# Eight-layer network on one core: a third product block on GpSimd, runs of 32 tokens in the recurrence, and the expert choice in three pieces

## The chip, the cores and the metric

The kernel runs on one core of a Trainium2 chip. Times are device microseconds of one execution of the whole program; less is better.

## The reference

The program computes four layers on a tensor `x` of 4 images, 128 channels and 64 x 64 pixels. Each layer adds a token mixer and then a feed-forward part to `x`: involution and recurrence; deformable convolution and an expert layer; convolution and an expert layer; attention and a top-2 expert layer. The change touches three of these eight stages.

```
# involution: normalised input xn, 7 x 7 taps, dilation 2, 8 groups of 16 channels
r = w_reduce @ xn + b_reduce                       # 32 channels
k = w_span @ r + b_span                            # 49 taps x 8 groups, per pixel
x[c, p] += sum over taps t of  k[t, group(c), p] * xn[c, p + 2 * offset(t)]

# recurrence over the 4096 tokens of each image (as the kernel computes it)
u = batchnorm(W @ layernorm(x))
y[t] = sigmoid(u[t] + V @ y[t - 1]);   x += y

# top-2 experts: 8 experts of 128 x 128, the two best of a token, weighted by a softmax over the two
x += sum over the two best e of  share_e * (expert_w[e].T @ layernorm(x) + expert_b[e])
```

## The kernel before, in words

`x` stays in SBUF all the time as `xs`, 128 channels on the partitions by 4 x 4096 tokens. The eight stages run one after the other. Inside the stages that matter here, a manual schedule fixes the order of PE (TensorE), ACT (ScalarE), DVE (VectorE) and POOL (GpSimd): each engine does its instructions in the order in which the Python code emits them. DMAs are issued from the SP queue.

**Involution.** The 49 taps are treated as 14 units of up to 4 taps: unit 2i holds 4 taps of row i (128 partitions: 4 taps x 32 channels), unit 2i+1 the other 3 (96 partitions). The picture is cut into 16 bands of 16 rows (1024 pixels), and each unit covers the 128 channels in 4 blocks of 32. In `make` (L293) PE expands the reduced channels to tap weights for one block (`inv_pk`, L302, four 512-column matmuls of 32 rows for two blocks), into one of three PSUM buffers. Three of the four blocks are then multiplied with the shifted image `inv_seen` by the DVE in one instruction that also adds the bias (L319); block 1 goes to ACT, which adds the bias (L316), and then to GpSimd, which multiplies (L317). So GpSimd multiplies two of the eight blocks of a pair of units. The products `inv_prod` are in 8 buffers. In `add` (L330) PE sums the taps of the four blocks with a folding matrix into `inv_out` (L333), for half of the pixels at a time. The loop emits, for each unit: blocks 0 and 1; the sums of the unit before for half 0; blocks 2 and 3; the sums of the unit before for half 1. After a band's last unit the DVE adds `inv_out` to `xs` (L355; L361 for the last band). All fp32 matmuls appear twice in the profile, as two passes. The tap weights `wtap` are spread to 16 channels by one DVE copy of 7168 columns before the loop (L285).

**Recurrence.** `layernorm` (L65, with `centred` at L69) centres 512-token chunks (L82), copies them to `rnn_xn` (L84), squares them (L86) and sums the squares (L91) for all 32 chunks; then one square root (L99) and one reciprocal (L100), and 32 products (L115) with the spread-out factor (L107). Then come the batch statistics (L389, L390) and the coefficients (L392 to L404). The sequence is computed in parallel runs: 4096 tokens are cut into runs of `LEN` = 64 tokens, all runs step together, and a first sweep over the last `WARM` = 20 tokens of each run makes the states from which the runs start. A step is, for each of two groups of two images, one matmul with `vt` (L456, 128 columns) onto the prepared input and one sigmoid (L461). The inputs are prepared for `BLK` = 4 steps at once by a matmul (L439) that reads `rnn_xn` at every 64th token. The first sweep makes 20 steps, the last 64, and in the last the DVE adds the results to `xs` (L467). A check of the norm of V (L415 to L427) decides whether a loop between the two sweeps runs; with this input it doesn't.

**Top-2 experts.** The 32 chunks are taken as 8 quads of 4, and each chunk in two halves of 4 experts, so a quad has 8 halves. For a half, `gated` (L1710) spreads four gates to all partitions (L1718, `top_pw`, four PSUM buffers) and the DVE multiplies the chunk by each (L1724, `top_xg`); PE then multiplies by the expert matrices (L1742, `top_po`, after a product with the biases at L1740 in each first half). The gates of a half are emitted one half ahead of its expert matmuls. The next quad's gates are prepared beside it by the generator `prepare` (L1672), which is advanced once a half: it centres, squares, makes the router's scores, and calls `choose` (L1637), 25 small DVE instructions and two of ACT in one piece. The step after that emits nothing, and the next one the transposes of the gates (L1704) with the copy `top_gt` (L1706).

## Time and profile before

| what | value |
|---|---|
| time, median of 3 runs | 8871.85 us (8869.74 to 8875.66) |
| the profiled execution's own time | 8533.12 us |
| its span | 8531.3 us |
| PE, DVE, ACT, POOL busy | 92%, 66%, 42%, 58% |
| involution's tap loop | 151.8 to 1221.8 us |
| recurrence | 1221.8 to 1490.0 us |
| top-2 experts | from about 8075 us to the end |

Lines with an L name a line of the kernel before. A group's line has the line, engine, operation, output and inputs, shape and count, then busy time and mean ns of one, then the idle time of the engine ahead of it and who ended it. A line of the timeline has the start, the duration of the run of equal instructions, the engine, and in brackets the idle time before it and who ended that. A wait's line has who waited for whom, then the sum, the count and the longest. PEld is PE's loading of weights.

### The profile page before, as it was taken

To read this page: it belongs to the slowest core of one execution; us is meant where nothing else is said; L and a number is where in the kernel's file an instruction comes from. 1 tells how busy PE (TensorE), PEld (TensorE's weight loads), DVE (VectorE), ACT (ScalarE), POOL (GpSimd) and SP (SyncE) were. 2 spreads that over 40 slices of the span, in tenths; PEclk is the share of its full clock that TensorE was granted. 3 is DMA by queue.
4 is the path that set the end of the run, shared out by engine and by line. 5 is a ranking of instruction groups with operands and counts; after the bars stand their busy time and mean duration, and the time that the engine had idled before them with its cause. 6 is when DMAs were issued, how large, how long until landed. Compare 5 with 4: busy or idle time off the path is not lost.

```text
span 8531.3 us, 146057 instructions
## 1 busy us (share of the span) xinstructions
PE 7867.6 (92%) x59834; PEld 3483.4 (41%) x59834; DVE 5591.7 (66%) x8297; ACT 3623.6 (42%) x6855; POOL 4943.6 (58%) x2479
## 2 busy tenths in 40 slices
PE   8999998677786688988999999999999999999899
PEld 2333324455555554443444344443444434444233
DVE  5777764688888843226676676776777667677155
ACT  2222222344444441040555555555555555555411
POOL 1444430477777710000888788887888878888600
PEclk8999998899999999997999999999999999999999
DMA  5333310688787723031455455454455544455400
GB/s 182 77 84 71 70 25 4 171 246 237 219 249 208 209 82 131 1 130 40 97 111 110 96 108 108 102 108 106 98 111 107 108 100 105 107 104 110 89 19 21
DMA packets 300201, 951.19 MB, mean 111 GB/s; under 512 B 41925, under 2 KB 114693, under 8 KB 241669
## 3 DMA queue, kind: packets, MB, share of 16 engines
q0 software_dynamic: 142848, 671.18, 33.4%
q1 hardware_dynamic: 156676, 270.60, 10.8%
q8 instruction: 472, 7.73, 0.4%
q14 instruction: 205, 1.67, 0.1%
HBM read 466.83 MB, written 72.17 MB: 63 GB/s over the span
## 4 chain that ended last, share of the span: by engine, by line
PE 55%; DVE 3%; issue 1%; DMA 1%; ACT 1%; POOL 0%; SPq 0%; DVEq 0%; ACTq 0%; POOLq 0%
PE att_pv L1444 15%; PE att_sc L1531 13%; PE att_mx L1388 10%; PE att_sc L1432 5%; PE conv_po L1198 3%; PE top_po L1742 3%; PE top_pw L1718 1%; DVE att_most L1399 1%; DMA moe_w<-in_L_ffn_weight 1%; PE att_sc L1361 0%; PE att_sc L1492 0%; PE att_sc L1475 0%; PE att_mx L1286 0%; PE att_sc L1322 0%; PE moe_acc L995 0%
## 5 line engine op out<-in xcount | busy, mean ns | idle before, releaser
L1463 POOL TENSOR_TENSOR att_acc<-att_acc,att_ex 128x2048 f32<-128x2048 f32 x640 | 2902.1, 4535 | 639.0 <-ACT att_ex L1532 619.7
L1399 DVE TENSOR_REDUCE att_most<-att_mx 128x2 f32<-128x1024 f32 x2016 | 2462.2, 1222 | 1071.7 <-PE att_mx L1388 990.8
L1532 ACT ACTIVATE att_ex<-att_sc 128x512 f32<-128x512 f32 x4096 | 2223.7, 594 | 1772.7 <-PE att_sc L1531 1488.1
L1531 PE MATMUL att_sc<-att_q,att_k 32*128 32x512 f32 x8192 | 2456.6, 606 | 0.0
L1388 PE MATMUL att_mx<-att_k,att_q 32*128 32x512 f32 x8064 | 2293.1, 647 | 12.9 <-DVE att_parts L1411 10.8
L1432 PE MATMUL att_sc<-att_rows,att_ones_b 32*128 32x256 bf16 (+1 forms) x6144 | 1502.6, 306 | 4.8 <-ACT att_ex L1532 4.7
L708 POOL DMA_INDIRECT dcn_g<-dcn_table,dcn_idx x1152 | 1100.0, 955 | 434.9 <-DMA dcn_g<-dcn_table,dcn_idx 119.9
L1444 PE MATMUL att_pv<-att_ex,att_vals 128*32 128x256 f32 x16384 | 1310.3, 391 | 0.0
L319 DVE SCALAR_TENSOR_TENSOR inv_prod<-inv_pk,bspan,inv_seen 128x1024 f32<-128x1024 f32 (+1 forms) x672 | 822.2, 1275 | 228.2 <-PE inv_pk L302 228.2
L1388 PEld LDWEIGHTS att_mx<-att_k,att_q 32*128 32x128 f32 x8064 | 611.1, 185 | 867.5 <-issue 707.2
L317 POOL TENSOR_TENSOR inv_prod<-inv_seen,inv_prod 128x1024 f32<-128x1024 f32 x224 | 528.4, 2359 | 679.1 <-ACT inv_prod L316 533.8
L1444 PEld LDWEIGHTS att_pv<-att_ex,att_vals 128*32 128x32 f32 x16384 | 322.6, 108 | 1319.7 <-issue 1301.5
L749 PE MATMUL dcn_pt<-ident,dcn_sum 128*128 128x128 f32 x2304 | 520.4, 310 | 336.3 <-DVE dcn_sum L733 335.9
L1531 PEld LDWEIGHTS att_sc<-att_q,att_k 32*128 32x128 f32 x8192 | 818.6, 183 | 11.0 <-issue 8.3
L722 ACT ACTIVATE dcn_one<-dcn_g,dcn_w 128x128 f32<-128x128 f32 x1152 | 456.3, 401 | 724.1 <-DMA dcn_g<-dcn_table,dcn_idx 719.2
L302 PE MATMUL inv_pk<-inv_red,wtap 32*96 32x512 f32 (+1 forms) x3584 | 605.7, 637 | 7.8 <-DMA inv_seen<-inv_image 7.8
L316 ACT ACTIVATE inv_prod<-inv_pk,bspan 128x1024 f32<-128x1024 f32 x224 | 249.2, 1113 | 820.9 <-PE inv_pk L302 811.8
L749 PEld LDWEIGHTS dcn_pt<-ident,dcn_sum 128*128 128x128 f32 x2304 | 374.7, 204 | 419.1 <-DVE dcn_sum L733 417.9
L333 PE MATMUL inv_out<-inv_prod,inv_fold 96*32 96x512 f32 (+1 forms) x3584 | 505.8, 606 | 18.3 <-DVE xs L355 18.3
L748 PE MATMUL dcn_pt<-ident,dcn_one 128*128 128x128 f32 x2304 | 477.4, 291 | 18.1 <-ACT dcn_one L722 18.1
L748 PEld LDWEIGHTS dcn_pt<-ident,dcn_one 128*128 128x128 f32 x2304 | 400.0, 205 | 228.3 <-issue 151.2
L725 DVE TENSOR_SCALAR dcn_part<-dcn_g,dcn_w 128x128 f32<-128x128 f32 x1152 | 405.6, 352 | 120.5 <-DMA dcn_g<-dcn_table,dcn_idx 87.7
(329 smaller groups left out, 7419.2 us busy)
## 6 DMA issues: line engine op xcount, KB each, us to landing
att_sum<-att_ex POOLq DMA_DIRECT2D x320, 1024.0 KB, 7.3
inv_seen<-inv_image SPq DMA_DIRECT2D x256, 266.0 KB
moe_w<-in_L_ffn_weight SPq DMA_DIRECT2D x64, 1024.0 KB
dcn_table<-dcn_xt SPq DMA_DIRECT2D x64, 512.0 KB
att_sum<-att_ex SPq DMA_DIRECT2D x32, 1024.0 KB
att_sum<-att_acc POOLq DMA_DIRECT2D x32, 1024.0 KB, 7.1
dcn_g<-dcn_table,dcn_idx POOLq DMA_INDIRECT x1152, 3.7
inv_image<-inv_rows SPq DMA_DIRECT2D x32, 304.0 KB
```

The costliest lines, as they stand in the source:

```text
L302: nc.tensor.matmul(pk[0:m, h, :], wtap[rg, unit, blk, 0:m], red[rg, h * CH : (h + 1) * CH], start=True, stop=True,)
L319: nc.vector.scalar_tensor_tensor(out=of, in0=pk[0:m].rearrange("p h (r x) -> p (h r) x", x=W), scalar=by, in1=view, op0=ALU.add, op1=ALU.mult,
L708: nc.gpsimd.indirect_dma_start(out=g, out_offset=None, in_=rows, in_offset=bass.IndirectOffsetOnAxis(ap=idx[:, j + i, k : k + 1], axis=0),)
L748: nc.tensor.matmul(out, one_, net.ident, start=i == 0, stop=False)
L749: nc.tensor.matmul(out, s, net.ident, start=False, stop=i == 3)
L1388: nc.tensor.matmul(pm[i] if alone else pm[:, i, :], q[r, t * P : (t + 1) * P], ks[r, kc * CH : (kc + 1) * CH], start=True, stop=True,)
L1399: nc.vector.tensor_reduce(most[:, 2 * half : 2 * half + 2, kc], pm, AX.X, ALU.max)
L1432: nc.tensor.matmul(pe[:, cols], ones_b[r], lows[g][r, cols], start=cols.start == 0, stop=False)
L1444: nc.tensor.matmul(block["pv"][r, cols], vals[b][:, t, r], ex[:, h, cols], start=t == 0 and half == 0, stop=t == NT - 1 and half == 1,)
L1463: nc.gpsimd.tensor_add(block["acc"], block["acc"], ex)
L1531: nc.tensor.matmul(pe, ks[r, t * P : (t + 1) * P], qs[c][r], start=False, stop=True)
L1532: nc.scalar.activation(ex[:, h, :], pe, AF.Exp)
```

## The change

- In the involution, block 3 of every odd unit goes the way of block 1, over ACT and GpSimd. So GpSimd multiplies three of the eight blocks of a pair of units. There are 10 product buffers. The sums are emitted half a unit later: half 0 of unit u after blocks 2 and 3 of unit u+1, half 1 after blocks 0 and 1 of unit u+2. The add into `xs` follows the sum that closes a band. The tap weights are two tiles, one for each kind of unit; the DVE fills the first by four copies, GpSimd the second by four.
- In the recurrence a run has 32 tokens, so there are twice as many, and a step has 256 columns for each group; `BLK` is 2, so an input matmul still has 512 columns. `rnn_xn` is stored with the token's place in the run outermost: the input matmul reads adjacent words, and the layernorm's copies, squares and products step by 2 KiB from word to word. The layernorm is the one with a variance for each image (`normed`, L119), whose products for one image are emitted among the copies of the next. The check of V's norm comes first, the statistics run over places in the run, and all of this is under the manual schedule. The starting states are cleared by GpSimd.
- In the top-2 stage `choose` is a generator in three pieces, one for each half. The transposes of the gates are emitted one half later than before.

```diff
-    return t.rearrange("p (r w) -> p r w", w=W) if len(like.shape) == 3 else t
+    return t.rearrange("p (r w) -> p r w", w=like.shape[2]) if len(like.shape) == 3 else t
...
-        wtap = sb.tile([P, UNITS * BLOCKS * TAPS * 2, 16], F32, name="wtap", bufs=1)
-        nc.vector.tensor_copy(wtap, wspan.unsqueeze(2).to_broadcast(list(wtap.shape)))
-        wtap = wtap.rearrange("p (u n m) c -> p u n (m c)", u=UNITS, n=BLOCKS)
+        wspan = wspan.rearrange("p (i f n m) -> p i f n m", i=K, f=2, n=BLOCKS)
+        wtap = [sb.tile([P, K, BLOCKS, 2 * t, 16], F32, name=f"wtap{t}", bufs=1) for t in (4, 3)]
+        for half, eng in enumerate((nc.vector, nc.gpsimd)):
+            m = 2 * (TAPS - half)
+            for blk in range(BLOCKS):
+                eng.tensor_copy(
+                    wtap[half][:, :, blk], wspan[:, :, half, blk, 0:m].unsqueeze(3).to_broadcast([P, K, m, 16])
+                )
+        wtap = [t.rearrange("p i n m c -> p i n (m c)") for t in wtap]
...
-                        wtap[rg, unit, blk, 0:m],
+                        wtap[half][rg, i, blk],
...
-                prod = sb.tile([P, 2, CH], F32, name="inv_prod", tag="inv_prod", bufs=8)
+                prod = sb.tile([P, 2, CH], F32, name="inv_prod", tag="inv_prod", bufs=10)
...
-                if blk == 1:
+                if blk == 1 or (blk == 3 and half):
...
+            if unit == UNITS - 1 and h == 1:
+                nc.vector.tensor_add(to, to, po.rearrange("p h t -> p (h t)"))
...
                 for unit in range(UNITS):
-                    prods = make(unit, seen, red, 0)
-                    if before:
-                        add(*before[0:3], 0)
-                    prods += make(unit, seen, red, 1)
-                    if before:
-                        add(*before[0:3], 1)
-                        if before[0] == UNITS - 1:
-                            nc.vector.tensor_add(before[3], before[3], before[1].rearrange("p h t -> p (h t)"))
-                    before = (unit, po, prods, net.xs[:, b, r * SPAN : (r + 1) * SPAN])
+                    prods = []
+                    for n in range(2):
+                        prods += make(unit, seen, red, n)
+                        if len(late) > 1:
+                            add(*late.pop(0))
+                    to = net.xs[:, b, r * SPAN : (r + 1) * SPAN]
+                    late += [(unit, po, prods, to, h) for h in range(2)]
...
-        xn = sb.tile([P, B, N], F32, name="rnn_xn")
-        net.layernorm(range(B), 1e-5, lambda b, c: xn[:, b, c * CH : (c + 1) * CH], sb, ps, 3)
...
-        LEN, WARM, MOST, BLK = 64, 20, 1.05, 4
+    LEN, WARM, MOST, BLK = 32, 20, 1.05, 2
...
+        xn = sb.tile([P, LEN, B, SEGS], F32, name="rnn_xn")
...
-            nc.vector.memset(e, 0.0)
+            nc.gpsimd.memset(e, 0.0)
...
+        with tc.manual_schedule(engines=ORDERED):
+            pt = bank()
+            nc.tensor.matmul(pt[:, 0:P], vt, vt, start=True, stop=True)
+            nc.vector.tensor_reduce(norm, pt[:, 0:P], AX.X, ALU.add, apply_absolute_value=True)
+            parts = [
+                net.normed(
+                    b, 1e-5, lambda c, b=b: xn[:, :, b, c * PART : (c + 1) * PART].rearrange("p t s -> p s t"), sb, bank
+                )
+                for b in range(B)
+            ]
+            for _ in range(NCH + 1):
+                next(parts[0])
...
+            for b in range(1, B):
+                for n in range(NCH):
+                    next(parts[b])
+                    if n % 2:
+                        next(parts[b - 1], None)
+                next(parts[b])
+            for _ in parts[B - 1]:
+                pass
+            for t in range(LEN):
+                statistics(t)
...
-                        if i == g + 1 and t0 + BLK < LEN:
+                        if i == 0 and t0 + BLK < LEN:
...
             most0, hit0 = first_best(lg, 0)
+            yield
...
             nc.scalar.activation(share1, share1, AF.Exp)
+            yield
...
-            choose(pt, g)
-            yield
+            yield from choose(pt, g)
             yield
```

## The prediction

> **What bounds the kernel now.** I read the page first (slices, chain, groups), then the busy time by stage, and inside each touched stage the timeline and the waits. The page's chain of work that ended last is 55% PE, spread over many stages that run one after the other; the change touches three of them, so each is read by itself. The busy time by stage (start:end, length, then busy us of PE, PEld, DVE, ACT, POOL, then the clock):
>
> ```profile
> core 0: us, PE busy (x) PEld busy (x) DVE busy (x) ACT busy (x) POOL busy (x), PEclk, DMA share, GB/s
> 151.80:1221.80 1070.00, 1050.49 (x7168) 321.67 (x7168) 839.74 (x692) 249.22 (x224) 528.43 (x224) 0.99 0.30 68
> 1221.80:1308.10 86.30, 81.28 (x192) 29.08 (x192) 45.12 (x67) 19.80 (x33) 0.00 (x0) 0.82 0.01 3
> 1380.10:1490.00 109.90, 97.81 (x320) 47.25 (x321) 38.78 (x32) 41.86 (x128) 1.06 (x2) 0.98 0.01 1
> 8193.50:8248.70 55.20, 52.27 (x169) 20.40 (x169) 28.49 (x62) 8.36 (x14) 0.00 (x0) 0.94 0.05 19
> ```
>
> These are the involution's taps, the recurrence's layernorm, its last sweep, and one of eight quads of the top-2 stage. A busy PE hides its waits here, as matmuls overlap their successors. One involution unit, from the timeline:
>
> ```profile
> 302.94 0.30 PEld L333 LDWEIGHTS inv_out<-inv_prod,inv_fold 128*32 128x32 f32 x8 [0.79 <-issue]
> 304.08 1.31 PE L302 MATMUL inv_pk<-inv_red,wtap 32*96 32x512 f32 x8
> 304.31 2.36 POOL L317 TENSOR_TENSOR inv_prod<-inv_seen,inv_prod 96x1024 f32<-96x1024 f32 x1 [2.30 <-ACT inv_prod L316]
> 305.23 3.66 DVE L319 SCALAR_TENSOR_TENSOR inv_prod<-inv_pk,bspan,inv_seen 96x1024 f32<-96x1024 f32 x3 [0.99 <-PE inv_pk L302]
> 305.32 0.16 PEld L333 LDWEIGHTS inv_out<-inv_prod,inv_fold 128*32 128x32 f32 x8 [0.79 <-issue]
> 307.62 0.27 PEld L333 LDWEIGHTS inv_out<-inv_prod,inv_fold 96*32 96x32 f32 x8 [0.76 <-issue]
> ```
>
> Two units take 9.33 (302.94 to 312.28 two units on). The DVE idles 1 us in each, though nearly all of its products are wanted at once: a loop. Block 3's product ends just after the sum group at 302.94 began, so that group takes 1.14 where the other takes 1.00; then comes the next group at L302, and only then the DVE's block 2. At a band's end the sums wait for the add into `xs`:
>
> ```profile
> PE inv_out L333 <- DVE xs L355: 18.3, 15, 1.2
> ```
>
> The adds are (1156.7-226.0)/14 = 66.48 apart, which is 7 x 9.33 and 1.2. The recurrence by groups (count | busy, mean ns):
>
> ```profile
> L439 PE MATMUL rnn_py<-rnn_xn,rnn_wt 128*128 128x512 f32 x84 | 79.1, 1033 | 4.3 <-PEq L475 4.3
> L461 ACT ACTIVATE rnn_y<-rnn_py,rnn_shift 128x128 f32<-128x128 f32 x166 | 54.3, 365 | 91.5 <-PE rnn_py L456 87.3 <-PE rnn_py L439 4.1
> L467 DVE TENSOR_TENSOR xs<-xs,rnn_y 128x512 f32<-128x512 f32 x32 | 39.8, 1296 | 105.8 <-ACT rnn_y L461 105.8
> L84 DVE COPY rnn_xn<-ln_d 128x512 f32<-128x512 f32 x32 | 22.1, 691 | 26.9 <-PE ln_d L82 26.9
> L115 DVE TENSOR_TENSOR rnn_xn<-rnn_xn,ln_r 128x512 f32<-128x512 f32 x32 | 20.2, 684 | 11.8 <-PE ln_r L107 11.8
> ```
>
> L439 reads every 64th token (256-byte steps): 1033 ns, where L82 with the same shape and adjacent words has 617. In top-2, PE waits for the DVE, which is inside the choice from 8240.50 to 8247.4, and then runs at half clock:
>
> ```profile
> 8193.48 3.86 PE L1718 MATMUL top_pw<-top_gt,ident 32*128 32x512 f32 x8 [2.94 <-DVE top_xg L1724]
> 8197.27 5.95 PE L1742 MATMUL top_po<-top_xg,top_we 128*128 128x512 f32 x8
> 8209.14 1.14 PE L1718 MATMUL top_pw<-top_gt,ident 32*128 32x512 f32 x8
> 8210.21 3.70 PE L1742 MATMUL top_po<-top_xg,top_we 128*128 128x512 f32 x8
> ```
>
> **What the Trainium skill says.** (1) "Vector Engine (DVE) Microarchitecture Reference", 5.2 Measured stream behaviour on trn2: fp32 words that aren't adjacent in pairs slow a stream, from 1.05 ns a column to 1.71 with dst hopping 4 KiB, 1.98 with all streams hopping, 2.5 at small steps. L467 (256-byte steps in and out) agrees: 1296/512 = 2.53. (2) "SBUF — State Buffer", SBUF: two separate sides: GpSimd and the DVE exclude each other on a shared port pair when the DVE is in a two-port mode or has two SBUF inputs. L319 has one input in PSUM and keeps 1270 to 1284 ns beside GpSimd: agrees. (3) "TensorE: Matmul & The Clock Gate", Part 1: an idle window of some 3.4 us halves PE's clock. Agrees: 1.00 before 1272, 0.50 from 1279 to 1308 after the reciprocal's gap.
>
> **Part 1, involution.** In odd units block 3 goes to ACT (1.11) and GpSimd (2.36). Per two units: DVE 5 x 1.2 = 6.0, GpSimd 3 x 2.36 = 7.1, both under PE's 9.2. Sums come half a unit later, so no product is late: block 3 by GpSimd is done 0.8 before its sum group. What waits next are the three `inv_pk` buffers: the last tile of a unit reuses that of its first, free after 1.13 (matmuls) + 0.05 + 1.27 (DVE) + 0.05 = 2.5, 0.24 into the second group; after an even unit, with DVE blocks 2, 3, 0 in a row, 0.36. Laid out with the trace's durations, the groups at L302 take 1.27, 1.30, 1.24, 1.39 and four sum groups 1.00 each: 9.19, so 0.14 x 112 = 16 less. At the band's end the add (1.21) stands behind one product of an odd unit, which has only two on the DVE; the sum wait falls from 1.2 to 0.1: 1.1 x 15 = 16. The old order laid out the same way gives 66.45 a band (measured 66.48), the new 64.4. **-32**, ends 0 (loop persists) and -60 (no buffer wait). The tap copy, 3.89 once, becomes four of 0.55 on the DVE and four on GpSimd, which may exclude each other: -1.7 to +1.5, taken as 0. Ten product buffers cover the longer life. POOL's two memsets (L432 before) end far before sweep 1.
>
> **Part 2, recurrence.** Layernorm: 32 copies and 32 products now step 2 KiB. The trace has no such step; between unchanged (0.69, 0.68) and L467's 2.53 a column (1.45, 1.30) I take the page's hop prices: 512 x 1.71 + 0.16 = 1.03 (0.16 is what 0.691 leaves over 512 x 1.05) and 512 x 1.98 + 0.15 = 1.16, as 2 KiB is nearer 4 KiB than 256 bytes. 32 x 2.19 = 70; four reciprocals (3.35) where one was, 13.4; waits for the four variances some 6 (2.49 before), 2 before the last products; PE's first matmul needs `rnn_vt`, issued at 1221.53 as third of the queue, some 2.5 later (gamma, issued at 1222.0, released ACT at 1223.83), 1.2 to the first copy: 95, and 3 for half clock: 98 against 86.3, **+12** (ends -8, PE's own work; +45, the 2.53 price and half clock). Squares read SBUF in steps: ACT is busy 20 of 86. Statistics: same 32 of 0.70, 0. Sweeps: the inputs at L439 become adjacent reads, and a pass of 512 adjacent columns takes 0.43 (weights of L82 load at 1222.43, 1222.86, 1223.29): two passes 0.86, where 1.70 stood (1349.57 to the next matmul at 1351.27). Four old steps of 64 runs take 6.71 (1355.10 to 1361.81) and become two steps of 128 runs, with the same two inputs. PE's order is then group 0 (0.43), inputs (0.86), group 1 (0.43), inputs (0.86), so that group 0's second step starts at 2.58; its result can be read 0.74 later (0.52 in the trace for 128 columns, and two passes longer by 0.11), the sigmoid of 256 takes 0.47 (0.365 for 128, and for 128 more an estimate of 0.8 ns each, between 0.6 from 365 at 128 and 597 at 512 and 1.0 from 597 at 512 and 1114 at 1024), the handover 0.06: 3.85. Last sweep: 15 x 3.85 + 2.5 + 4.2 = 64.5 for 108.7, -44; the first keeps its 20 steps, now 9 x 3.85 + 2.5 = 37.2 for 32.7, +5. **-39**, ends -28 and -45. The DVE's adds (2 x 1.3 in each 3.85) stay hidden; what is late next is PE itself, 2.58 + 0.86 of 3.85.
>
> **Part 3, top-2.** A quad takes 55.2; an undisturbed half takes 5.56 with the bias product (8203.58 to 8209.14) and 4.70 without (8209.14 to 8213.84), so eight take 41.0; the next quad's preparation adds 3.4 (two pairs of L1678), 1.9 and 2 x 0.5: 47.3. So 7.9 is lost, as the wait of 2.9, the `top_pw` group of 3.86 for 1.07 and the half clock after it, and that in each of seven quads. Pieces of 2.6, 2.0, 2.0 stand behind four products each (2.5): three halves hold 15.3 of DVE for 15.9 of PE, so no half runs over. The last piece makes the gates one half later; the next quad's first `top_pw` now waits for the copy `top_gt`: 1.0, and 0.2 of buffers. (7.9 - 1.2) x 7 = **-47**, ends -15 and -55.
>
> No DMA is added or moved on SP's queue, and the stages between recurrence and top-2 keep their order and only start earlier.
>
> Sum: -32 + 12 - 39 - 47 = **-106**. The profiled execution took 8533.1 (span 8531.3), so 8427. The timed median is 8871.9, 339 more, and no view shows where; I carry microseconds: **8766**.
>
> **Rivals.** A (0.2): steps at 2.53 and half clock in the layernorm: +45 for +12, 8799. For it: L467, and 0.50 from 1279; against: cents and sums mix now. B (0.12): the pieces only move the DVE's lateness by a half (15.3 against 15.9 is thin): -15 for -47, 8798. C (0.1): the involution's loop just turns through the buffers: 0 for -32, 8798. D, slower (0.04): GpSimd runs slower with three products, as it and the DVE meet. Laid out, 2.6 us changes nothing, 3.0 gives 67.1 a band, 3.5 gives 74.1: 16 x 7.6 = +122, with the rest (-74) +48: 8920. It decides from about 3.3. Against: 2337 to 2376 in 224 products.
>
> **Numbers.** Main case 0.54. The range joins A and B (-41: 8831) above, the layernorm's and the involution's lower ends (-154: 8718) below. 0.2% (18 us) is what a measurement can tell. D and mishaps leave 0.04 slower, 0.03 same.
>
> **What would show it.** Adds into `xs` 64.4 apart; strided copies near 1.03; 3.85 per two steps; no quad over 49; GpSimd at 2.36. Adds still 66.5 apart, copies at 1.45, or quads at 53 would refute a part.

## The result, and the profile after

The changed kernel takes 8755.65 us (median of 4 runs, 8751.33 to 8762.93), the kernel before 8870.8 us (4 runs, 8866.48 to 8875.66): a ratio of 0.9871, with a 95% interval of 0.9854 to 0.9888, or 115 us less. The forecast was 8766 us, in a range of 8718 to 8831. The profiled execution took 8758.54 us, with a span of 8756.7.

In the table, each stage goes from and to the same event in both profiles: the involution from its first `inv_pk` matmul to the end of its last add into `xs`, the layernorm from there to the end of its last product, a sweep from its first input matmul to its last sigmoid or last add into `xs`. The whole recurrence ends where the next stage begins, which is 1 us before its last add ends.

| stage | before | after | change | predicted |
|---|---|---|---|---|
| involution, tap loop | 1070.0 | 1030.5 | -39.5 | -32 |
| tap copy before it (start of the loop) | 151.8 | 149.3 | -2.5 | 0 |
| recurrence, layernorm | 87.1 | 103.8 | +16.7 | +12 |
| recurrence, first sweep | 33.8 | 38.4 | +4.6 | +5 |
| recurrence, last sweep | 110.9 | 65.7 | -45.2 | -44 |
| recurrence, whole | 268.2 | 244.0 | -24.2 | -27 |
| top-2 experts | 455.7 | 409.8 | -45.9 | -47 |
| deformable convolution | 1553 | 1891 | +338 | 0 |
| everything between it and top-2 | 5032 | 5032 | 0 | 0 |

The stages that the change touches give -112 in these two profiles, the measured medians -115. The row of the deformable convolution is no effect of the change; it is taken up at the end.

The busy time by stage, of the kernel after (start:end, length, then busy us of PE, PEld, DVE, ACT, POOL, then the clock): the tap loop, the layernorm, the last sweep, one quad.

```profile
core 0: us, PE busy (x) PEld busy (x) DVE busy (x) ACT busy (x) POOL busy (x), PEclk, DMA share, GB/s
149.30:1179.80 1030.50, 1025.98 (x7168) 280.86 (x7168) 718.46 (x583) 373.67 (x336) 794.04 (x342) 0.99 0.32 72
1179.80:1283.70 103.90, 86.68 (x196) 25.19 (x196) 79.74 (x72) 36.06 (x36) 0.00 (x0) 0.81 0.01 2
1358.90:1423.70 64.80, 61.31 (x192) 35.60 (x192) 34.73 (x32) 29.67 (x64) 0.69 (x1) 0.97 0.00 1
8514.50:8562.90 48.40, 47.73 (x169) 18.71 (x170) 27.94 (x61) 8.36 (x14) 0.00 (x0) 1.00 0.06 23
```

POOL's work in the tap loop has grown by half. PE does the same matmuls in 39.5 us less, and is busy for nearly all of the stage in both kernels (1026 of 1030.5 us, 1050 of 1070). In the layernorm the DVE went from 45 us of work to 80. The quad now runs at full clock (1.00, where the quad of before had 0.94).

The timeline of the tap loop, two units of it, without the weight loads: PE before, then PE, DVE and POOL after, with some lines left out. A group of L302 or L308 makes the taps of two blocks, a group of L333 or L340 is the sums of one half.

```profile
302.94 1.21 PE L333 MATMUL inv_out<-inv_prod,inv_fold 128*32 128x512 f32 x8
304.08 1.31 PE L302 MATMUL inv_pk<-inv_red,wtap 32*96 32x512 f32 x8
305.32 1.06 PE L333 MATMUL inv_out<-inv_prod,inv_fold 128*32 128x512 f32 x8
306.32 1.37 PE L302 MATMUL inv_pk<-inv_red,wtap 32*128 32x512 f32 x8
307.62 1.18 PE L333 MATMUL inv_out<-inv_prod,inv_fold 96*32 96x512 f32 x8
308.73 1.34 PE L302 MATMUL inv_pk<-inv_red,wtap 32*128 32x512 f32 x8
310.01 1.06 PE L333 MATMUL inv_out<-inv_prod,inv_fold 96*32 96x512 f32 x8
311.00 1.34 PE L302 MATMUL inv_pk<-inv_red,wtap 32*96 32x512 f32 x8
```

```profile
299.70 1.23 PE L308 MATMUL inv_pk<-inv_red,wtap 32*128 32x512 f32 x8
300.86 1.06 PE L340 MATMUL inv_out<-inv_prod,inv_fold 128*32 128x512 f32 x8
300.88 1.28 DVE L325 SCALAR_TENSOR_TENSOR inv_prod<-inv_pk,bspan,inv_seen 128x1024 f32<-128x1024 f32 x1 [1.13 <-PE inv_pk L308]
...
301.86 1.48 PE L308 MATMUL inv_pk<-inv_red,wtap 32*128 32x512 f32 x8
303.03 3.67 DVE L325 SCALAR_TENSOR_TENSOR inv_prod<-inv_pk,bspan,inv_seen 128x1024 f32<-128x1024 f32 x3 [0.88 <-PE inv_pk L308]
303.27 1.06 PE L340 MATMUL inv_out<-inv_prod,inv_fold 96*32 96x512 f32 x8
304.27 1.21 PE L308 MATMUL inv_pk<-inv_red,wtap 32*96 32x512 f32 x8
305.40 1.07 PE L340 MATMUL inv_out<-inv_prod,inv_fold 96*32 96x512 f32 x8
...
306.40 1.46 PE L308 MATMUL inv_pk<-inv_red,wtap 32*96 32x512 f32 x8
306.71 7.13 POOL L323 TENSOR_TENSOR inv_prod<-inv_seen,inv_prod 96x1024 f32<-96x1024 f32 x3 [1.95 <-ACT inv_prod L322]
...
307.79 1.06 PE L340 MATMUL inv_out<-inv_prod,inv_fold 128*32 128x512 f32 x8
...
308.78 1.23 PE L308 MATMUL inv_pk<-inv_red,wtap 32*128 32x512 f32 x8
```

Two units take 9.08 (299.70 to 308.78), where they took 9.33. From start to start, the four groups of taps take 5.09 together, as they did before (5.10). The four groups of sums take 1.00 each, where two of the four took 1.14 and 1.11: no sum waits for a product any more, and that is the whole gain of the steady loop. POOL's three products fill 7.13 of the 9.08 and still wait for ACT.

What is left of the loop are the two groups of taps that take 1.46 and 1.48 where the others take 1.2. There are three `inv_pk` buffers and two blocks to a group, so the second block of a group takes the buffer of the first block of the group before. For the group at 301.86 the DVE frees it at 302.16, by the single product of 300.88, and the matmuls of the second block begin at 302.21; for the group at 306.40 it is the last product of the row of three, which ends at 306.70, and the second block begins at 306.75.

The adds into `xs` are 63.75 us apart, which is 7 x 9.08 and 0.2: the wait of 1.2 at a band's end is all but gone as well.

The recurrence by groups, after:

```profile
L469 PE MATMUL rnn_py<-rnn_xn,rnn_wt 128*128 128x512 f32 x104 | 54.1, 609 | 4.5 <-PEq L505 4.1 <-DVE rnn_wt L460 0.4
L491 ACT ACTIVATE rnn_y<-rnn_py,rnn_shift 128x256 f32<-128x256 f32 x102 | 47.2, 475 | 55.8 <-PE rnn_py L486 55.8
...
L162 DVE TENSOR_TENSOR rnn_xn<-rnn_xn,rnn_pd 128x512 f32<-128x512 f32 x32 | 36.4, 1191 | 6.6 <-PE rnn_pd L158 6.6
...
L144 ACT ACTIVATE ln_sq<-rnn_xn 128x512 f32<-128x512 f32 x32 | 33.3, 1079 | 55.0 <-DVE rnn_xn L142 55.0
...
L142 DVE COPY rnn_xn<-rnn_pd 128x512 f32<-128x512 f32 x32 | 30.9, 1022 | 8.8 <-PE rnn_pd L140 8.8
...
L152 DVE RECIPROCAL ln_rstd<-ln_rstd 128x512 f32<-128x512 f32 x4 | 13.4, 3353 | 5.9 <-ACT ln_rstd L151 5.9
```

The input matmuls fell from 1033 ns to 609; copies and products rose from 691 and 684 to 1022 and 1191, near the estimates (1.03 and 1.16 us). The squares, which now read `rnn_xn` in steps, rose from 597 to 1079. The top-2 stage after, at the end of one quad and the start of the next:

```profile
8550.98 1.61 PE L1750 MATMUL top_pw<-top_gt,ident 32*128 32x512 f32 x8
...
8552.52 3.70 PE L1774 MATMUL top_po<-top_xg,top_we 128*128 128x512 f32 x8
...
8556.15 1.14 PE L1750 MATMUL top_pw<-top_gt,ident 32*128 32x512 f32 x8
...
8562.89 1.14 PE L1750 MATMUL top_pw<-top_gt,ident 32*128 32x512 f32 x8 [0.68 <-ACT top_gt L1738]
```

The group of 3.86 that stood behind a wait of 2.9 is one of 1.61 without an idle time, and the expert matmuls after it keep 3.70. The new wait for the copy `top_gt` is there, with 0.68. Quads are 48.42 apart.

### The profile page after: what moved, and what is told of

The parts are those of the page before. It is cut to its first block, busy times and chain, and to the rows that moved or that the text cites. A ratio compares the mean times of both kernels' runs of the same rounds, so it can differ in the third digit from the quotient of the medians.

```text
span 8756.7 us, 145965 instructions
## 1 busy us (share of the span) xinstructions
PE 7848.4 (90%) x59726; PEld 3477.4 (40%) x59726; DVE 5504.4 (63%) x8189; ACT 3671.7 (42%) x6906; POOL 5215.4 (60%) x2597
## 4 chain that ended last, share of the span: by engine, by line
PE 54%; DVE 2%; issue 1%; DMA 1%; ACT 1%; POOL 0%; SPq 0%; DVEq 0%; ACTq 0%; POOLq 0%
PE att_pv L1474 14%; PE att_sc L1561 12%; PE att_mx L1418 10%; PE att_sc L1462 4%; PE conv_po L1228 3%; PE top_po L1774 3%; PE top_pw L1750 1%; DVE att_most L1429 1%; DMA moe_w<-in_L_ffn_weight 1%; PE att_sc L1391 0%; PE att_sc L1522 0%; PE att_sc L1505 0%; PE top_po L1772 0%; PE att_mx L1316 0%; PE moe_acc L1025 0%
## 5 line engine op out<-in xcount | busy, mean ns | idle before, releaser
L323 POOL TENSOR_TENSOR inv_prod<-inv_seen,inv_prod 128x1024 f32<-128x1024 f32 x336 | 790.0, 2363 | 233.8 <-ACT inv_prod L322 225.0
L325 DVE SCALAR_TENSOR_TENSOR inv_prod<-inv_pk,bspan,inv_seen 128x1024 f32<-128x1024 f32 (+1 forms) x560 | 697.5, 1279 | 307.3 <-PE inv_pk L308 307.3
L799 PE MATMUL dcn_out<-dcn_st,dcn_wk 128*128 128x512 f32 x576 | 385.0, 756 | 415.2 <-ACT dcn_st L795 406.4
L322 ACT ACTIVATE inv_prod<-inv_pk,bspan 128x1024 f32<-128x1024 f32 x336 | 373.7, 1112 | 654.9 <-DVE inv_prod L325 373.8
L308 PE MATMUL inv_pk<-inv_red,wtap 32*96 32x512 f32 (+1 forms) x3584 | 608.2, 636 | 6.3 <-DMA inv_red<-inv_reds 4.4
L795 ACT COPY dcn_st<-dcn_pt 128x512 f32<-128x512 f32 x288 | 167.1, 580 | 1057.9 <-remote 742.7
L778 PEld LDWEIGHTS dcn_pt<-ident,dcn_one 128*128 128x128 f32 x2304 | 440.4, 224 | 275.6 <-issue 197.0
L778 PE MATMUL dcn_pt<-ident,dcn_one 128*128 128x128 f32 x2304 | 516.6, 310 | 31.1 <-ACT dcn_one L752 19.1
L763 DVE SCALAR_TENSOR_TENSOR dcn_sum<-dcn_g,dcn_w,dcn_part 128x128 f32<-128x128 f32 x1152 | 354.5, 345 | 291.0 <-remote 202.6
L340 PE MATMUL inv_out<-inv_prod,inv_fold 96*32 96x512 f32 (+1 forms) x3584 | 478.6, 605 | 1.4 <-POOL inv_prod L323 1.0
```

Of the source, the lines that this page charges most:

```text
L308: nc.tensor.matmul(pk[0:m, h, :], wtap[half][rg, i, blk], red[rg, h * CH : (h + 1) * CH], start=True, stop=True,)
L323: nc.gpsimd.tensor_mul(of, view, of)
L325: nc.vector.scalar_tensor_tensor(out=of, in0=pk[0:m].rearrange("p h (r x) -> p (h r) x", x=W), scalar=by, in1=view, op0=ALU.add, op1=ALU.mult,
L778: nc.tensor.matmul(out, one_, net.ident, start=i == 0, stop=False)
```

## The experiments

Since the stages run one after the other, an experiment in one stage is read from that stage's own window, in one profiled execution. How much a stage differs between profiles is seen in kernels that leave it as the change made it: the tap loop takes 1030.3 to 1030.9 us in five such experiments, the layernorm 101.0 to 104.0 in nine kernels, the two sweeps together 104.1 to 106.8, the whole recurrence 243.6 to 246.8, the top-2 stage 409.8 to 411.4. Each kernel is the changed one with the edit shown; the ratios are to the kernel before, on the same chip.

### Which half of the involution's change brings the gain

```diff
-                if blk == 1 or (blk == 3 and half):
+                if blk == 1:
```

> The changed kernel, but block 3 of the odd units goes back to the VectorE (two blocks of eight on GpSimd, sums still half a unit late). The involution's stage, from its first inv_pk matmul to the end of the last add into xs, is 1030.5 us in the changed kernel and 1070.0 in the one before. Theory 1: what the old loop lost were sums that waited for the last product, and sums half a unit late cure that alone. The hand timetable of the prediction, which gives 1036.2 for the changed kernel, gives 1034.7 here: so the stage stays within 3 us of 1030.5, with the VectorE at 6 x 1.28 of 9.1 us per two units. Theory 2: the third block on GpSimd brings the gain, because the VectorE's products were too many: then the stage goes back to 1060 to 1070.

Measured: the stage takes 1029.1 us, the adds are 63.75 apart; ratio 0.9882 (0.9865 to 0.9898). The third block on GpSimd brings nothing; the late sums do it without it. The two tap tiles and the ten product buffers stay in all these kernels and were not tried apart; but the groups of taps, which read the tiles, are no shorter than before (5.09 for 5.10), so the tiles are not where the steady loop gains. By groups, in this kernel:

```profile
L325 DVE SCALAR_TENSOR_TENSOR inv_prod<-inv_pk,bspan,inv_seen 128x1024 f32<-128x1024 f32 (+1 forms) x672 | 823.6, 1277 | 182.4 <-PE inv_pk L308 182.4
...
L323 POOL TENSOR_TENSOR inv_prod<-inv_seen,inv_prod 128x1024 f32<-128x1024 f32 x224 | 528.7, 2360 | 492.8 <-ACT inv_prod L322 492.8
```

The DVE has 824 us of products in 1029 and still waits 182 for PE. With three blocks it had 698 and waited 307: what is taken from it turns into idle time, one for one.

The other half alone:

```diff
-                        if len(late) > 1:
+                        if len(late) > 0:
```

> The changed kernel, but each unit's sums stand where they stood before the change (right after the products of the next unit's first and second half, no half unit later); three blocks of eight stay on GpSimd. Theory 1: block 3 by way of ScalarE and GpSimd is done 1.1 + 2.4 us after its taps instead of 1.3, so the sums behind it wait: the timetable gives 1216.6 for the stage against 1036.2 with late sums, +180 us, and the whole kernel is slower than before the change (about 8935). Theory 2 (the VectorE's load is what counts): the stage is at most 1045.

Measured: the stage takes 1223.4 us (+193 over the changed kernel), the ratio is 1.0093 (1.0076 to 1.0109), slower than before the change. The wait for GpSimd is that of one group of sums in each pair of units, the odd unit's for half 0:

```profile
509.60 1.06 PE L340 MATMUL inv_out<-inv_prod,inv_fold 96*32 96x512 f32 x6
...
511.08 1.05 PE L340 MATMUL inv_out<-inv_prod,inv_fold 96*32 96x512 f32 x2 [0.42 <-POOL inv_prod L323]
512.06 1.14 PE L308 MATMUL inv_pk<-inv_red,wtap 32*128 32x512 f32 x8
```

The group takes 2.46 us, up to 512.06, where 1.00 is usual: its last two matmuls are the sums of block 3. A pair of units takes 10.68 instead of 9.08, and the wait of 1.2 at a band's end is back.

So the third block isn't merely useless without the late sums, it costs: the product by way of ACT and GpSimd takes 1.1 + 2.4 where the DVE takes 1.3, and the sums stood right behind it. The half unit of delay hides that and the DVE's lateness with one edit.

### Where GpSimd becomes the bound

```diff
-                if blk == 1 or (blk == 3 and half):
+                if blk in (1, 3):
```

> The changed kernel with block 3 of the even units on GpSimd too: four of eight. GpSimd needs 4 x 2.36 = 9.44 us for two units, over the 9.08 that the changed kernel takes. Theory 1: GpSimd becomes the bound, 9.44 x 112 = 1057 and the ends, so the stage takes about 1060 (timetable 1063 where it gives 1036 for three), +30 us. Rival: the VectorE, with 4 x 1.28 of 9.1, is relieved further and the inv_pk buffers come free sooner: the stage falls below 1030.

Measured: 1051.1 us, +21; ratio 0.9911 (0.9891 to 0.9931). The expected direction and cause:

```profile
L323 POOL TENSOR_TENSOR inv_prod<-inv_seen,inv_prod 128x1024 f32<-128x1024 f32 x448 | 1039.9, 2381 | 4.6 <-ACT inv_prod L322 4.5
```

GpSimd waits 4.6 us in the whole stage: it is the bound. The expected 1060 was high, because a pair of units cost 9.28 (64.99 between adds, over 7) and not 4 x 2.36: in this kernel's timeline products that follow each other without a wait overlap a little, 14 of them in 32.61 us, which is 2.33 each. A product's own mean stays at 2.36 to 2.38 whether GpSimd has 224, 336 or 448 products, beside a DVE that reads PSUM: the prediction's rival D, that the two slow each other, has nothing for it here.

### What is left of the tap loop: three tries that failed

```diff
-                if blk == 1 or (blk == 3 and half):
+                if blk == (0 if half else 2) or (blk == 2 and half):
```

> The changed kernel, still three of eight blocks on GpSimd and late sums, but other ones: block 2 of even units, blocks 0 and 2 of odd ones, instead of block 1 of each and block 3 of odd ones. The VectorE then has at most two products in a row instead of three. Theory: what the changed loop still loses is the wait for an inv_pk buffer behind three VectorE products in a row (two groups of taps of eight matmuls take 1.4 us where the others take 1.15, in each two units); the timetable gives 1016.2 against 1036.2: the stage falls by about 20 us to 1010. Rival: the groups of 1.4 us have another cause (weight loads of 128 columns, or reading the taps), and the stage stays at 1030 within 4.

Measured: 1025.8 us, -4.7 instead of -20; ratio 0.9879 (0.9862 to 0.9895). The expectation was wrong about its own edit: block 3 of an odd unit and blocks 0 and 1 of the next are three DVE products in a row again, and the timeline shows that row at 3.80 us. One group of taps of 1.65 replaced the one of 1.48.

```diff
-                pk = ps.tile([P, 2, CH], F32, name="inv_pk", tag="pk", bufs=3)
+                pk = [ps.tile([P, CH], F32, name="inv_pk", tag="pk", bufs=6) for h in range(2)]
...
-                    nc.scalar.activation(prod[0:m], pk[0:m], AF.Identity, bias=by)
+                    for h in range(2):
+                        nc.scalar.activation(prod[0:m, h], pk[h][0:m], AF.Identity, bias=by)
```

The DVE's product is cut in two in the same way.

> The changed kernel, but the taps' results lie in six PSUM tiles of 512 columns instead of three of 1024, and the VectorE and ScalarE work on each half by itself (20 and 12 instructions of 512 columns in two units instead of 10 and 6 of 1024; GpSimd's products stay at 1024). Choosing other blocks for GpSimd took only 5 of the 20 us that the timetable promised, as three VectorE products still stood in a row there. Theory: two of the four groups of taps in two units (9.08 us) wait some 0.25 to 0.3 for a buffer behind such a row; a half comes free 0.6 us sooner, so these waits go: 8.55 to 8.75 for two units, the stage 985 to 1000 instead of 1030.5. The VectorE then needs 10 x 0.74 = 7.4 of it. Rival: the smaller products add so much on the VectorE (0.2 us each for starting) that it is late, and the stage stays at 1025 or more.

Measured: 1063.0 us, +32; ratio 0.9919 (0.9902 to 0.9935). The rival is right on the sign, though not on its reason: the DVE still waits 270 us for PE in the stage. Two DVE halves take 1.40 where one product took 1.28, two on ACT 1.26 where one took 1.11. So the second half of a buffer comes free later than the whole did, and a group's last half block waits for it, as the weight loads of one group show:

```profile
302.58 0.25 PEld L308 LDWEIGHTS inv_pk<-inv_red,wtap 32*96 32x96 f32 x6 [0.84 <-DVE inv_prod L328]
303.19 0.24 PEld L308 LDWEIGHTS inv_pk<-inv_red,wtap 32*96 32x96 f32 x2 [0.36 <-DVE inv_prod L328]
```

The 0.84 ahead of the first line is only the time in which PE does the sums, and such a stretch stands ahead of every group of taps, in the changed kernel too; the 0.36 inside the group is the wait.

```diff
-                if blk == 1 or (blk == 3 and half):
+                if blk == 1:
```

on top of the tiles of 512 columns:

> The same with the tiles of 512 columns, but two blocks of eight on GpSimd instead of three (with tiles of 1024 this made no difference: 1029.1 us for the stage against 1030.5). Theory: the VectorE then has 12 halves of 0.7 to 0.74 in two units, 8.4 to 8.9, as much as TensorE needs, so here the third block on GpSimd counts: the stage is 10 to 40 us longer than with three blocks. Rival: the number of blocks on GpSimd makes no difference here either (within 4 us).

Measured: 1061.4 us; ratio 0.9918 (0.9899 to 0.9938). The rival holds: the number of GpSimd's blocks makes no difference here either, with 12 x 0.743 = 8.9 of DVE work in 9.34 for two units. So the loop isn't filled by the DVE's work; with the waits inside the groups, this says that it turns at the pace of the way from PE's group to a product to the freed buffer and back to PE. A third edit of this loop rides in the last experiment.

### The recurrence, taken apart

```diff
+        net.layernorm(
+            range(B), 1e-5,
+            lambda b, c: xn[:, :, b, c * PART : (c + 1) * PART].rearrange("p t s -> p s t"), sb, ps, 3,
+        )
-            parts = [
-                net.normed(
...
```

> The changed kernel, but the recurrence's layernorm is the one of before (all four images at once, one reciprocal, squares on ScalarE read from PSUM), writing xn with the new steps of 2 KiB; the check of vt stands behind it. The stage from the end of the last add into xs to the last product of the layernorm takes 103.9 us in the changed kernel, 86.3 before. Theory 1: the first half is bound by TensorE as before (50.4), the reciprocal and its wait take 7, and 32 stepped products of 1.19 make 38: 95.5, so of the 17.6 us that the changed kernel lost here about half are the four reciprocals and the wait for vt, and half the steps. Theory 2: the steps alone cost it all: 102 to 104.

Measured: the layernorm takes 96.4 us (expected 95.5), the recurrence 237.2; ratio 0.9868 (0.984 to 0.9897). With the old form the steps cost 9.3 us (96.4 for 87.1). In this kernel the copies at 1.03 hide beside PE's work (the DVE waits 22 us for PE among them), and only the products set the pace:

```profile
L115 DVE TENSOR_TENSOR rnn_xn<-rnn_xn,ln_r 128x512 f32<-128x512 f32 x32 | 35.8, 1187 | 2.2 <-PE ln_r L107 2.2
...
L84 DVE COPY rnn_xn<-ln_d 128x512 f32<-128x512 f32 x32 | 30.6, 1032 | 22.1 <-PE ln_d L82 22.0
```

Next, runs of 32 with the old order of `rnn_xn`, which the layernorm and the statistics follow:

```diff
-        xn = sb.tile([P, LEN, B, SEGS], F32, name="rnn_xn")
+        xn = sb.tile([P, B, N], F32, name="rnn_xn")
+        toks = xn.rearrange("p b (s t) -> p t b s", t=LEN)
...
-                py, wt, xn[:, t : t + BLK, g * PAIR : (g + 1) * PAIR, :], start=True, stop=True
+                py, wt, toks[:, t : t + BLK, g * PAIR : (g + 1) * PAIR, :], start=True, stop=True
```

> The changed kernel with runs of 32 tokens, but xn lies token after token as before: copies and products of the layernorm are adjacent words, and the sweeps' inputs read every 32nd token (128-byte steps). Theory 1: such a read costs TensorE twice, at 128 bytes as at 256 (1.70 us for the two passes instead of 0.86): two steps then take 5.5 us instead of 3.85, the first sweep 52 instead of 38.4, the last 90 instead of 64.8: +39; the layernorm falls from 103.9 to about 91; in all the recurrence takes 27 us more. Theory 2: the number of steps made the gain, not the order of xn: the sweeps stay at 3.85 per two steps, and the recurrence is 12 us shorter.

And the new order with the old runs of 64:

```diff
-    LEN, WARM, MOST, BLK = 32, 20, 1.05, 2
+    LEN, WARM, MOST, BLK = 64, 20, 1.05, 4
```

> The changed kernel with runs of 64 tokens in fours, as before, but with xn by place in the run (steps of 1 KiB in the layernorm, the sweeps' inputs adjacent); the statistics then take 64 matmuls of 256 columns instead of 32 of 512. Theory 1: the adjacent inputs made the sweeps' gain: four steps take 2.16 for TensorE with both inputs (two steps of 0.22 and two inputs of 0.86) and three more steps of 0.95 each, 5.0 where before the change they took 6.71: the first sweep 24 us (38.4 changed, 32.7 before), the last 79 (64.8 changed, 108.7 before), together 103 as in the changed kernel. Theory 2: half as many steps made the gain: the last sweep stays at 100 or more. Copies of the layernorm at 1 KiB steps: within 0.1 of the 1.02 at 2 KiB if the size of the step does not matter.

Measured, with the ratios 0.9905 (0.9877 to 0.9934) and 0.9881 (0.9852 to 0.991):

| kernel | runs | inputs | layernorm | first sweep | last sweep | recurrence |
|---|---|---|---|---|---|---|
| before | 64 | every 64th | 87.1 | 33.8 | 110.9 | 268.2 |
| rec_rows | 32 | every 32nd | 89.2 | 55.6 | 91.7 | 271.4 |
| rec_runs64 | 64 | adjacent | 101.2 | 27.0 | 84.9 | 250.1 |
| changed | 32 | adjacent | 103.8 | 38.4 | 65.7 | 244.0 |
| rec_one_norm | 32 | adjacent | 96.4 | 38.4 | 65.7 | 237.2 |

The input matmuls of rec_rows and of rec_runs64:

```profile
L471 PE MATMUL rnn_py<-rnn_xn,rnn_wt 128*128 128x512 f32 x104 | 97.3, 1031 | 4.7 <-PEq L507 4.3 <-DVE rnn_wt L461 0.4
```

```profile
L470 PE MATMUL rnn_py<-rnn_xn,rnn_wt 128*128 128x512 f32 x84 | 46.0, 641 | 4.7 <-PEq L506 4.3 <-DVE rnn_wt L461 0.4
```

A step of 128 bytes costs PE as much as one of 256 (1031 and 1033 ns). Shorter runs alone bring nothing: the two sweeps take 147.3 us together where they took 144.7, since there are more inputs to read at the double price. The adjacent inputs alone bring 32.8, and with them the shorter runs bring 7.8 more, or 5 by the profiles in which the changed sweeps take 106.8. Two steps of rec_rows take 5.56 (expected 5.5), four of rec_runs64 5.0 (expected 5.0), so PE's order of steps and inputs is a sound way to price a sweep; the sweeps' sums for rec_runs64 were 9 too low, as the ends of a sweep were sized too small. The layernorm's loss is no sum of two parts: the form with four variances alone costs 2.1 (rec_rows, 89.2 for 87.1), the steps alone 9.3, and both together 14 to 17 (101.0 to 104.0). The layernorm's copies take 1.02 at steps of 1 KiB as at 2 KiB; the products take 1.26 there, 1.19 at 2 KiB.

### The choice in top-2

```diff
-            yield from choose(pt, g)
+            for _ in choose(pt, g):
+                pass
+            yield
+            yield
```

> The changed kernel, but the choice stands in one piece again, in the half in which its first piece stands now; the gates' transposes stay one half later than before the change. The stage of top-2 takes 409.8 us changed, 455.7 before, its quads 48.4 and 55.2. Theory 1: what a quad lost was the VectorE inside 6.9 us of choice, ahead of the products that TensorE needs; it comes back whole: quads of 55 to 56, the stage about 458, +48 us. Theory 2: the later gates (no wait of the transposes for the choice) make the gain: quads of at most 50.

Measured: the stage takes 462.2 us, quads of 55.1 to 56.6; ratio 0.9933 (0.991 to 0.9955). The stall is back as it was, 2.94 and then a group of 3.86, as in the lines of before at 8193.48:

```profile
8238.05 3.86 PE L1753 MATMUL top_pw<-top_gt,ident 32*128 32x512 f32 x8 [2.94 <-DVE top_xg L1759]
```

The other edit keeps the pieces and puts the gates' transposes back into the half of the last piece:

```diff
             yield from choose(pt, g)
-            yield
             pg = bank("pd")
```

> The changed kernel with the choice in three pieces, but the transposes of the gates stand in the half of the last piece, as before the change, instead of one half later. Theory 1: TensorE, in order, then waits for the third piece, which stands behind four products: about 2 us a quad more, of which the 0.7 for the copy top_gt at the quad's start comes back: quads of 49.5 to 50.5, the stage 418 to 424. Theory 2: the later gates only cost (0.7 a quad for top_gt): the stage is 5 us shorter.

Measured: 417.2 us, quads of 49.45; ratio 0.9889 (0.9869 to 0.9908). PE, in order, waits for the last piece:

```profile
8505.04 0.63 PE L1735 MATMUL top_pd<-ident,top_gates 128*128 128x128 f32 x4 [1.58 <-DVE top_gates L1701]
```

The wait of 1.58 takes the place of the 0.68 for `top_gt`. With the later gates in place the pieces are worth 52 us of the stage. The later gates are worth 7 once there are pieces; without pieces they make the stage longer (462.2 against 455.7 before).

### The version that should have been better

```diff
-                if blk == 1 or (blk == 3 and half):
+                if blk in ((0, 3) if half else (1,)):
```

with the layernorm of rec_one_norm.

> The changed kernel with the two edits that could shorten it further: the layernorm of the recurrence from before the change with the new steps (6.8 us of the recurrence), and for GpSimd block 1 of even units and blocks 0 and 3 of odd ones. This choice, unlike the one tried before (block 2, then 0 and 2, where block 3 and the next unit's blocks 0 and 1 still made three), leaves at most two VectorE products in a row. Theory: rows of three hold an inv_pk buffer too long, 0.25 to 0.3 us twice in two units; the timetable gives 1026.2 for the stage where it gives 1036.2 for the changed kernel (measured 1030.5): 1015 to 1022 now, and the whole 15 to 22 us below the changed kernel. Rival: the loop turns through the three buffers whatever the rows: 1024 to 1031, and the whole 7 to 13 us below.

Measured: ratio 0.9875 (0.9858 to 0.9891), no better than the changed kernel's 0.9871. The recurrence takes 236.7 (-7.3), but the tap loop 1038.1 (+7.6). Neither theory holds. ACT's block 0 of the odd unit runs beside the DVE's row, so the DVE still does three products at a stretch, and two of the four groups of taps take 1.54 to 1.64 instead of 1.46 and 1.48:

```profile
304.56 3.77 DVE L325 SCALAR_TENSOR_TENSOR inv_prod<-inv_pk,bspan,inv_seen 128x1024 f32<-128x1024 f32 x3 [1.21 <-PE inv_pk L308]
305.90 0.25 PEld L308 LDWEIGHTS inv_pk<-inv_red,wtap 32*96 32x96 f32 x4 [0.19 <-DVE inv_prod L325]
```

The wait inside the group ends when the first product of the row does (305.84), and in the other long group it ends with a single product (300.00 to 301.27). So the row isn't what holds the buffer: as in the changed kernel, the second block of a group waits for the product of the first block of the group before. That fits the loop through the buffers of the prediction's rival C. Why this kernel needs 0.07 us more for two units (64.25 between adds, for 63.75) stays open.

The profile speaks for the changed kernel with the old layernorm alone, some 7 us less, which the interval of a timed comparison can't resolve.

## Why the prediction was right, by its steps

The sum was -106, the stages gave -112. Part of that closeness is luck, as two errors point opposite ways: the involution gained 7.5 us more than foreseen, by a mechanism of which one half did nothing, and the layernorm lost 4.7 more.

**Involution, -32 predicted, -39.5 measured.** The steady loop was mis-sized: 9.08 for two units, not 9.19. The four groups of taps take 1.16, 1.41, 1.13 and 1.39 from start to start, 5.09 in all, where the timetable had 1.27, 1.30, 1.24 and 1.39, 5.20 in all: those that wait for no buffer are shorter, and one that waits is longer. That makes 0.25 x 112 = 28 instead of 16. The wait at a band's end went as foreseen, 1.17 to 0.19 in each of 15 bands, 15 us; some 3 are given back in the first band, which the sum left out: its add comes 75.2 us after the loop's start, where it came 74.2 after it, though the units are shorter. In this band the sums begin half a unit later (2.3 us), and PE waits for the later tap copies. The reason given, that no product is late any more, was right, and so were the buffer waits that it foresaw in the second group of each unit. But the prediction put beside it a step that does no work: "In odd units block 3 goes to ACT and GpSimd". The runs give the whole gain to the late sums and nothing to the third block, at the band's end too, though the prediction leaned on the odd unit's two products there. Rival C named what is left, the loop through the buffers, and was wrong that it would keep everything.

**The tap copy, 0 predicted.** The table's -2.5 is no clean measure of it: the copies themselves begin anywhere between 146.3 and 150.4 us in these kernels, as the work ahead of them ends. Counted from the first copy, PE starts after 0.75 in each of the 13 profiles with the new copies, as it needs only the first of them, where it started after 3.95. But the price was mis-sized. The DVE's four copies take 3.74 us beside GpSimd's four, not four times 0.55:

```profile
148.55 3.74 DVE L289 COPY wtap<-wspan 128x896 f32<-128x896 f32 x4 [27.61 <-DMA inv_reds<-inv_rd]
148.68 4.08 POOL L289 COPY wtap<-wspan 128x672 f32<-128x672 f32 x4 [138.65 <-DMA inv_reds<-inv_rd]
```

The first DVE copy takes 0.69, each of the other three 1.09. That the two engines exclude each other, which the prediction allowed for, fits this; no run has the copies on one engine alone. The first add into `xs` ends up 75.97 us after the first copy, where it came 78.13 after it. Faster units make 1.8 of these 2.2, and half a unit of delay takes 2.3 back; so the copies in pieces are worth some 2.7, an estimate from these figures and more than the 1.7 that the prediction allowed. The gain comes from the early start, which it left out.

**Layernorm, +12 predicted, +16.7 measured** (14 to 17 over the nine kernels with this layernorm). The prices of the steps were right: 1.022 for 1.03, 1.191 for 1.16. They were estimates from the prices per column that the Trainium skill, "Vector Engine (DVE) Microarchitecture Reference", 5.2 Measured stream behaviour on trn2, gives for hops of 4 KiB (measured there with 32-bit integers), and the trace agrees at 2 KiB. Rival A, the price of small steps, is refuted. The mis-sized term is the DVE's waiting: it idles 24 of 104 us, 8.8 before copies, 6.6 before products, 5.9 before reciprocals and 2.8 at the start, where the sum had about 15 (its work is 80 where the sum had 84). Copies of one image and products of the one before share three PSUM banks, and PE fills them in order; that both engines therefore wait in turn is argued from the code, not tested. The older form, with the same steps, spends its copies under a busy PE.

**Sweeps, -39 predicted, -40.6 measured** (-38 by the profiles in which the two sweeps take 106.8). Two steps take 3.84, as laid out; the sigmoid of 256 columns takes 475 ns for the estimated 470. The sum of -27 for the recurrence became -24.2 through the layernorm.

**Top-2, -47 predicted, -45.9 measured.** Quads of 48.42 for 48.5; the 1.0 put down for `top_gt` is 0.68, the 0.2 for buffers 0.47 (1.61 less 1.14). Rival B, that the pieces only move the lateness, is refuted by the quads and by top_one_piece.

**The 339 us that "no view shows".** They lie in the deformable convolution, which the change doesn't touch. In the profiles of the two kernels it takes 1553 and 1891 us:

```profile
1490.00:3043.40 1553.40, 1166.09 (x6240) 794.90 (x6240) 1274.36 (x3706) 657.45 (x1560) 1110.38 (x1157) 0.92 0.76 219
```

```profile
1423.70:3314.70 1891.00, 1228.17 (x6240) 854.69 (x6240) 1284.93 (x3706) 571.55 (x1560) 1114.15 (x1158) 0.81 0.63 180
```

It is the same work on another chip. In the four experiments on one chip it takes 1551 to 1555, and the kernel before has a median of 8528 there; on a second chip 1887 to 1895, with 8869; on two more 1916 to 1922, with 8895 and 8901. So by these figures the profile of before came from a chip of the first sort and its timed runs from one of the second. Carrying microseconds, not a ratio, was right: the tap loop takes 1030.3 to 1030.9 on the first two of these chips alike. The total can't show it, as a ratio would have given 8762.

## What to carry to other kernels

When sums stand right behind the products that they need, a delay of half a round in the order can be worth all of what a rebalancing of engines promises; try the delay alone first, because the rebalancing may do nothing, or do harm without it. Here a matmul's moving operand that stepped over words cost PE 1033 ns for 609 at every read. Laying the data out for it, with runs of 32, saved the sweeps 40 to 43 us (147.3 in rec_rows) and cost the layernorm 12 to 15 (89.2 there). So it can be worth laying data out for the engine that reads it most and that sets the pace. Long strings of small instructions on one engine belong in pieces behind the work that another engine waits for, and their consumer one piece later still.

## What the hardware showed that was not expected

- The step of PE's moving operand: 512 columns take 1031 to 1038 ns in the profile at 128 and at 256 bytes, 609 to 641 when adjacent. The size of the step makes no difference between these two.
- ACT squares 512 columns in 597 ns from PSUM, 631 from adjacent SBUF words and 1078 with steps of 1 KiB or 2 KiB in SBUF.
- The deformable stage, with its gathers, takes 1551 to 1555, 1887 to 1895 or 1916 to 1922 us on different chips, with the same program for the stage. In the profile of before, from the fast sort, ACT waits for gathers; in that of after its copies `dcn_st` start late, released by something that the trace only calls remote, while the DMA engines are less busy (a share of 0.63 instead of 0.76). The longest waits of ACT there, before and after:

```profile
ACT dcn_one L722 <- DMA dcn_g<-dcn_table,dcn_idx: 719.2, 900, 6.8
```

```profile
ACT dcn_st L795 <- remote: 742.7, 79, 20.5
```

What the remote release is stays open; no run here changes it.
